# A graph network on one core: half of a comparison matrix moved from VectorE to ScalarE in every fourth tick of the first convolution, and one index write moved with it

## The chip, the core and the metric

The kernel runs on one core of a Trainium2 chip. The metric is the device time in microseconds (us) of one execution; the kernel before was timed in 3 runs. A core has five engines with a queue each, and each works its queue strictly in the order in which the program issued it: TensorE (PE, with its weight loads shown as PEld), VectorE (DVE), ScalarE (ACT), GpSimd (POOL) and SyncE (SP), the last of which only issues DMAs here.

## The reference

There are 12500 nodes with 64 features and 200000 edges, sorted by destination. Two graph convolutions over the nodes come first (a mean over the incoming edges, two 64x64 products, a bias), then a message step over the edges, whose results are averaged by `src`.

```python
h = jnp.maximum(_layernorm(x), 0.0)
agg = jax.ops.segment_sum(h[src], dst, num_segments=N)       # first convolution
cnt = jax.ops.segment_sum(jnp.ones(E), dst, num_segments=N)
h = relu(agg / maximum(cnt, 1)[:, None] @ W1l.T + b1 + h @ W1r.T)
...                                                          # second convolution, the same without relu
x = x + out
h = jnp.maximum(_layernorm(x), 0.0)
m = relu(concat([h[src], h[dst], edge_attr]) @ W1 + b1) @ W2 + b2
return x + segment_mean(m, src)
```

## The kernel before, in words

**Blocks and cells.** The nodes are cut into 49 blocks of 256. An edge belongs to a cell (destination block B, source block k), so there are 49 x 49 = 2401 cells, each with 128 slots. A sort (`sort(B)`, inside `made_cells`) puts the edges of destination block B into their cells. It runs on DVE and PE beside the first convolution, one block ahead, in 13 steps a block, which `sort_to` deals out by the number of cells done (about one step in a tick).

**Ticks of a convolution.** `some_cells` handles G = 4 cells, which this text calls a tick; a convolution has 601 ticks, the last with a single cell. A tick gathers source rows by multiplying a 0/1 matrix `turned` (made by DVE, L735) with the node table on PE (L890, tile `got`, four PSUM banks, two for a tick); ACT casts the result into `rows` (L894, two casts a tick). Then `hot` (L744, DVE) builds a second 0/1 matrix: for each of the four cells 256 columns, 1 where the slot's local destination number (`dcol`) equals the column. Three ticks later (`yield` three times) `Sums.add` multiplies `hot` by `rows` on PE (L769) into the block's sums `acc`.

**The end of a block.** When the 49 cells of a block are summed, `conv` goes on in the following ticks: ACT copies the sums (L810), DVE adds and scales them (L814 to L822), PE transposes them (L828), ACT copies the transposed block (L830, `both_t`), PE multiplies it by the weights in the next tick (L833), DVE adds the bias in the same tick (L835, `conv`), and ACT and DVE make the next table from that (L841 and L346 to L352).

**The order inside a tick.** For every engine the order of issue is: first the new tick's gather, casts and `hot`; then one step of each older tick and block in `line` (sums, `conv`); then the sort's steps (`sort_to`); then zeroing DMAs; then one step of `turned` for the next 16 cells; last a step of `edge_terms` (`beside`), which from cell 150 on computes the edge features' share of the messages: PE transposes (L402), an ACT copy (L408), PE products (L417), an ACT copy (L425, `terms_o`, three buffers), an ACT copy of positions (L379), and eight indirect DMAs on POOL (L385) that scatter the results to memory.

**The sort's positions.** In the sort's step with the first half of the products L639, DVE computes `pos_f` from the ranks (L644) and then writes it, scaled and as int32, to `pos` or `pos_late` (L645). Those positions are read by L379 only, many ticks later. In the next sort step ACT copies the products (L650, L651 to `scol`, L653 to `dcol`).

**The second convolution and the message stage** follow. The message stage already makes half of its own such matrices on ACT (`hot_a`): one `Abs` for each cell with the slot's number as bias (L1091), and one `Relu` over four cells (L1093), so that 1 - 2|column - number|, cut at zero, is 1 on equality and 0 elsewhere.

Of the kernel before, what the change touches and what calls it, by code (L numbers as in the profile page):

```python
# [12 lines left out]
AF = mybir.ActivationFunctionType  # L13
OP = mybir.AluOpType
# [100 lines left out]
def fast_path(  # L115
# [19 lines left out]
    nc = tc.nc  # L135
# [5 lines left out]
    NB = -(-N // BLK)  # L141
# [39 lines left out]
    G = 4  # L181
# [19 lines left out]
    for s, xs in enumerate(xs_all):  # L201
        full = min((s + 1) * CH, FULL) - s * CH
# [24 lines left out]
    every = consts.tile([P, 2 * P], BF, name="every")  # L227
# [18 lines left out]
    bias = []  # L246
# [50 lines left out]
    dcol = consts.tile([P, CELLS + 1], BF, name="dcol")  # L297
# [206 lines left out]
    def pos_of(B):  # L504
        return pos[:, B] if B < EARLY else pos_late[:, B - EARLY]
# [3 lines left out]
    def made_cells(work, psum):  # L509
# [60 lines left out]
        def pairs(a):  # L570
            return a.rearrange("p (g c) -> p g c", c=2)

        def mid(a, n):

            return a.unsqueeze(2).to_broadcast([a.shape[0], a.shape[1], n, 2])

        def lead_(a, n):

            return a.unsqueeze(1).to_broadcast([a.shape[0], n, a.shape[1], 2])

        def earlier(a, n):

            (row, _), (step, _) = a.ap
            return bass.AP(a.tensor, a.offset, [[row, P], [2 * step, TG], [2 * step, n], [step, 2]])

        def sort(B):

            keyed, shifted, slo, dlo = batch[B]
            kv = keyed[:, T:]
            odd = T // 2  # L590
            KE = NB + T - 1

            v = work.tile([P, TG, 3, NB, 2], BF, name="hot3", bufs=1)
            nc.vector.tensor_tensor(v[:, :, 0], mid(pairs(kv), NB), lead_(kexp, TG), op=OP.is_equal)  # L594
            yield
            p = psum.tile([P, 512], FT, name="pX")
            q = p[:, :2 * NB].rearrange("p (k c) -> p k c", c=2)
            for g in range(TG):
                nc.tensor.matmul(q, lead, v[:, g, 0], start=g == 0, stop=g == TG - 1)
            r = work.tile([P, TG, KE, 2], BF, name="ranks", bufs=1)  # L600
            nc.vector.tensor_tensor(r[:, :, NB:NB + odd], mid(pairs(kv), odd), earlier(shifted, odd), op=OP.is_equal)
            nc.vector.tensor_tensor(r[:, :, NB + odd:], mid(pairs(kv), T - 1 - odd),
                                    earlier(keyed[:, 2:], T - 1 - odd), op=OP.is_equal)
            yield
            nc.vector.tensor_mul(v[:, :, 1], v[:, :, 0], mid(pairs(slo), NB))
            yield
            ahead_p = work.tile([P, NB, 2], BF, name="ahead_p", bufs=1)
            with nc.allow_low_precision(reason="integers up to 256 are exact"):
                nc.vector.tensor_reduce(ahead_p, q.unsqueeze(2).to_broadcast([P, NB, 2, 2]), AX.X, OP.add)
            nc.vector.tensor_mul(r[:, :, 0:NB], v[:, :, 0], lead_(ahead_p, TG))  # L610
            yield
            nc.vector.tensor_mul(v[:, :, 2], v[:, :, 0], mid(pairs(dlo), NB))
            yield
            k = KE
            for n in range(3):
                h = k - k // 2
                nc.vector.tensor_tensor(r[:, :, 0:k - h], r[:, :, 0:k - h], r[:, :, h:k], op=OP.add)  # L617
                k = h
                if n == 1:
                    yield  # L620
            rb = work.tile([P, T], BF, name="rank_b", bufs=1)
            with nc.allow_low_precision(reason="integers up to 256 are exact"):
                nc.vector.tensor_reduce(pairs(rb), r[:, :, 0:k].rearrange("p g k c -> p g c k"), AX.X, OP.add)
            nc.vector.tensor_max(most, most, rb)
            halves = []
            for g0, g1 in ((0, (TG + 1) // 2), ((TG + 1) // 2, TG)):
                yield
                hot = work.tile([P, (TG + 1) // 2, S, 2], BF, name="hot_r")
                nc.vector.tensor_tensor(hot[:, :g1 - g0], mid(pairs(rb)[:, g0:g1], S), lead_(rexp, g1 - g0),  # L629
                                        op=OP.is_equal)  # L630
                halves.append((g0, g1, hot))
            yield
            p = psum.tile([P, 512], FT, name="pX")
            for g0, g1, hot in halves:
                yield

                for g in range(g0, g1):
                    for c in range(2):
                        nc.tensor.matmul(p[:, :2 * NB].rearrange("p (v k) -> p v k", v=2), hot[:, g - g0, :, c],  # L639
                                         v[:, g, 1:3, :, c], start=g + c == 0, stop=g + c == TG)  # L640
                if g0 == 0:
                    j, n, f = table_of(B)
                    q = work.tile([P, T], FT, name="pos_f", bufs=1)
                    nc.vector.scalar_tensor_tensor(q, rb, float(NB), kv, op0=OP.mult, op1=OP.add)  # L644
                    nc.vector.tensor_scalar(pos_of(B), q, float(n), float(n * NB + f),  # L645
                                            op0=OP.mult, op1=OP.add)
            n, f = place[B]
            F = len(order[n])
            cols = work.tile([P, 2 * NB], BF, name="cols_o")
            nc.scalar.copy(cols, p[:, :2 * NB])  # L650
            nc.scalar.copy(scol[:, scol_at[n]:scol_at[n] + NB * F].rearrange("p (k f) -> p k f", f=F)[:, :, f],  # L651
                           p[:, 0:NB])
            nc.scalar.copy(dcol[:, B * NB:(B + 1) * NB], p[:, NB:2 * NB])  # L653
            yield
            p = psum.tile([P, 512], FT, name="pX")
            pt = p.bitcast(BF)[:2 * NB, 0:S]
            nc.tensor.transpose(pt, cols, ident_b)
            o = work.tile([2 * NB, S], BF, name="rows_o", bufs=1)
            nc.scalar.copy(o, pt)
            nc.sync.dma_start(srow_b[B].rearrange("(k s) -> k s", s=S), o[0:NB])  # L660
            nc.sync.dma_start(srow_k[n][:, f * S:(f + 1) * S], o[0:NB])
            nc.sync.dma_start(drow_k[n][:, f * S:(f + 1) * S], o[NB:2 * NB])
            yield
# [19 lines left out]
        p = psum.tile([P, 512], FT, name="pX")  # L683
# [19 lines left out]
    with tc.tile_pool(name="raw_ps", bufs=1, space=bass.MemoryType.PSUM) as raw_ps:  # L703
        for n, raw in enumerate(raws):
            p = raw_ps.tile([P, D], FT, name="pW", bufs=2)
# [34 lines left out]
    def hot(work, cols, bufs, g=G):  # L740

        o = work.tile([P, g // 2, 2 * P, 2], BF, name="hot", bufs=bufs)
        n = cols.shape[1] // 2
        nc.vector.tensor_tensor(  # L744
            o[:, :n],
            cols.rearrange("p (g c) -> p g c", c=2).unsqueeze(2).to_broadcast([P, n, 2 * P, 2]),
            local.rearrange("p h q c -> p (h q) c").unsqueeze(1).to_broadcast([P, n, 2 * P, 2]),
            op=OP.is_equal)
        return o
# [44 lines left out]
    def even(a, z):  # L794
        return slice(a, z + (z - a) % 2)

    psum = ctx.enter_context(tc.tile_pool(name="sums_ps", bufs=2, space=bass.MemoryType.PSUM))
    sums = Sums(psum)
    layers = ExitStack()
    gather = layers.enter_context(tc.tile_pool(name="gather_ps", bufs=4, space=bass.MemoryType.PSUM))  # L800
    work = layers.enter_context(tc.tile_pool(name="layers", bufs=2))
# [79 lines left out]
    def some_cells(layer, t, c0, a, z):  # L881
        n = z - a
        table = (ta, tb)[layer]
        g = next_rows()
        for c in range(0, n, 2):
            m = min(2, n - c)
            p = gather.tile([P, 512], FT, name="got")
            for i in range(c, c + m):
                for h in range(2):
                    nc.tensor.matmul(p[:, (i - c) * D3:(i - c + 1) * D3],  # L890
                                     t[:, h, (a - c0 + i) * S:(a - c0 + i + 1) * S],
                                     table[:, (a + i) % NB, h], start=h == 0, stop=h == 1,
                                     skip_group_check=True)
            nc.scalar.copy(g[:, c:c + m, :D3], p[:, :m * D3].rearrange("p (c d) -> p c d", c=m))  # L894
        o = hot(work, dcol[:, even(a, z)], 5)
        yield
        yield
        yield
        full = []
        sums.add(o, g, a, z, lambda *a: full.append(a))  # L900
        for B, acc in full:
            yield from conv(layer, table, wcat[layer], bias[layer],
                            (after_conv1, after_conv2)[layer], B, acc)
# [67 lines left out]
    work = ctx.enter_context(tc.tile_pool(name="last", bufs=2))  # L971
# [186 lines left out]
    while summed:  # L1158
        f, args = summed.pop(0)
# [262 lines left out]
```

## Time and profile before

| what | value |
|---|---|
| median of 3 runs | 3682.99 us (3680.9 to 3687.05) |
| profiled execution | 3679.43 us, span of its instructions 3677.6 us |
| mean granted TensorE clock | 0.988 |
| first convolution, from its first gather to its last tick | 90.6 to 1306 us of the span |
| second convolution | to about 2275 us, message stage to the end |
| busy in the span | PE 93%, weight loads 92%, DVE 89%, ACT 68%, POOL 73% |

A busy share is a mean over stages. The lines by window, by waits and in order of time, which the prediction shows, say what holds each stage.

### The profile page before, as it was taken

How to read it: one execution, taken by the hardware profiler on the slowest of the kernel's cores; microseconds unless marked ns; L12 is line 12 of the kernel's file. 1: busy time of each engine (PE TensorE's matmuls, PEld its weight loads, DVE VectorE, ACT ScalarE, POOL GpSimd, SP SyncE). 2: the span in 40 equal slices, each digit the busy share in tenths (PEclk: the TensorE clock that was granted, in tenths of full speed). 3: DMA queues.
4: the chain of work that ended last, by engine and by line, in shares of the span. 5: the costliest groups of instructions: out<-in, count | busy, mean ns of one | idle time of the engine just before them, and what ended most of it. 6: DMA issues, size and time to landing. Idle time of an engine off the chain costs nothing.

```text
span 3677.6 us, 126942 instructions
## 1 busy us (share of the span) xinstructions
PE 3425.8 (93%) x50925; PEld 3367.7 (92%) x50925; DVE 3269.0 (89%) x5738; ACT 2506.9 (68%) x5949; POOL 2698.3 (73%) x2305
## 2 busy tenths in 40 slices
PE   1799999999899999999999998999999999999987
PEld 0788989898889999999999997999999999999887
DVE  7999999999999978788788787899889998998998
ACT  3455656565556667777777775788888888887665
POOL 4067787777777877777777773788888888887444
PEclk9999999999999999999999999999999999999999
DMA  6754545554454434444444444666766666666664
GB/s 211 268 164 150 169 152 163 155 161 151 147 168 145 128 125 142 132 137 147 136 131 137 140 134 144 224 214 200 218 212 211 204 214 214 207 207 206 194 211 140
DMA packets 413671, 635.66 MB, mean 173 GB/s; under 512 B 94131, under 2 KB 296247, under 8 KB 413070
## 3 DMA queue, kind: packets, MB, share of 16 engines
q1 hardware_dynamic: 353106, 572.87, 49.4%
q0 software_dynamic: 53312, 51.36, 4.1%
q8 instruction: 399, 6.54, 0.7%
q10 hardware_dynamic: 6652, 3.24, 0.4%
q14 instruction: 202, 1.65, 0.1%
HBM read 474.72 MB, written 155.83 MB: 171 GB/s over the span
## 4 chain that ended last, share of the span: by engine, by line
PE 64%; DVE 25%; DMA 5%; issue 3%; POOL 2%; SPq 1%; ACT 1%; DVEq 0%; ACTq 0%; POOLq 0%
PE acc L769 23%; PE got L890 13%; PE got L1071 12%; PE got L1072 6%; DVE hot L744 6%; DVE turned L735 4%; PE pE L417 3%; DVE hot_r L629 3%; PE pE L402 2%; DVE ranks L617 1%; DVE turned_d L735 1%; POOL terms L385 1%; DMA terms<-tb 1%; DMA terms_in<-terms 1%; DVE hot L594 1%
## 5 line engine op out<-in xcount | busy, mean ns | idle before, releaser
L385 POOL DMA_INDIRECT terms<-terms_o,turn_i x1666 | 1904.0, 1143 | 649.9 <-issue 427.8
L894 ACT CAST rows<-got 128x384 bf16<-128x384 f32 x2402 | 1038.4, 485 | 657.2 <-PE got L890 642.6
L769 PEld LDWEIGHTS <-hot 128*128 128x128 bf16 x12006 | 1032.5, 99 | 13.5 <-issue 4.0
L769 PE MATMUL acc<-rows,hot 128*128 128x193 bf16 x9604 | 1010.8, 248 | 0.0
L1083 POOL TENSOR_TENSOR hidden<-hidden 128x512 f32<-128x512 f32 (+1 forms) x602 | 756.4, 1256 | 265.1 <-ACT hidden L1080 179.5
L890 PEld LDWEIGHTS <-turned 128*128 128x128 bf16 x9604 | 814.6, 98 | 88.1 <-DVE turned L735 58.9
L744 DVE TENSOR_TENSOR hot<-dcol,local 128x1024 bf16<-128x1024 bf16 x1202 | 807.5, 682 | 9.0 <-PE acc L769 8.1
L735 DVE TENSOR_SCALAR turned<-srow,nid 128x2048 bf16<-128x2048 bf16 (+1 forms) x906 | 777.6, 872 | 20.7 <-issue 10.6
L1071 PE MATMUL got<-ta,turned 128*128 128x128 bf16 x3920 | 600.1, 221 | 7.3 <-DVE turned L735 7.3
L1071 PE MATMUL got<-tb,turned_d 128*128 128x128 bf16 x3920 | 600.6, 221 | 1.1 <-DVE turned_d L735 0.8
L890 PE MATMUL got<-ta,turned 128*128 128x192 bf16 x4802 | 510.5, 249 | 71.5 <-DVE turned L735 47.9
L1072 PE MATMUL got<-tb,turned_d 128*128 128x64 bf16 x3920 | 546.3, 193 | 0.0
L1072 PE MATMUL got<-ta,turned 128*128 128x64 bf16 x3920 | 546.1, 193 | 0.0
L1091 ACT ACTIVATE hot_a<-every,scol 128x256 bf16<-128x256 bf16 x1200 | 507.0, 493 | 0.0
L890 PE MATMUL got<-tb,turned 128*128 128x192 bf16 x4802 | 494.4, 246 | 0.9 <-DVE turned L735 0.5
L1080 ACT ACTIVATE hidden<-y 128x512 f32<-128x512 f32 (+1 forms) x301 | 190.4, 633 | 272.5 <-DVE y L1077 156.2
L1071 PEld LDWEIGHTS <-turned 128*128 128x128 bf16 x3920 | 362.1, 98 | 8.2 <-issue 7.8
L1071 PEld LDWEIGHTS <-turned_d 128*128 128x128 bf16 x3920 | 359.5, 98 | 1.7 <-DVE turned_d L735 1.7
L1072 PEld LDWEIGHTS <-turned 128*128 128x128 bf16 x3920 | 359.4, 98 | 1.2
L1072 PEld LDWEIGHTS <-turned_d 128*128 128x128 bf16 x3920 | 359.9, 98 | 0.0
L1093 ACT ACTIVATE hot_a<-hot_a 128x1024 bf16<-128x1024 bf16 x300 | 317.2, 1057 | 9.5
L735 DVE TENSOR_SCALAR turned_d<-drow,nid 128x2048 bf16<-128x2048 bf16 (+2 forms) x302 | 320.2, 1101 | 0.0
(217 smaller groups left out, 4898.1 us busy)
## 6 DMA issues: line engine op xcount, KB each, us to landing
srow<-srow_b SPq DMA_DIRECT2D x300, 512.0 KB
srow<-srow_k SPq DMA_DIRECT2D x149, 512.0 KB
drow<-drow_k SPq DMA_DIRECT2D x149, 512.0 KB
terms_in<-terms SPq DMA_DIRECT2D x294, 160.0 KB
edges<-in_edge_attr_dram SPq DMA_DIRECT2D x200, 192.0 KB
terms<-tb SPq DMA_DIRECT2D x200, 160.0 KB
terms<-tb SPq DMA_DIRECT2D x48, 640.0 KB
terms<-terms_o,turn_i POOLq DMA_INDIRECT x1666
```

The lines of the kernel that those rows point to most:

```text
L385: nc.gpsimd.indirect_dma_start(out=terms[j][:], out_offset=bass.IndirectOffsetOnAxis(ap=at[:, c, h:h + 1], axis=0), in_=o[:, c, h], in_off ...
L735: nc.vector.tensor_scalar(o[:, h, :n * S], r[:, :n * S], nid[:, h:h + 1], None, op0=OP.is_equal)
L744: nc.vector.tensor_tensor(o[:, :n], cols.rearrange("p (g c) -> p g c", c=2).unsqueeze(2).to_broadcast([P, n, 2 * P, 2]), local.rearrange(" ...
L769: nc.tensor.matmul(self.acc[B][:, h, :W3], lt, r[:, c, 0:W3], start=k + h == 0, stop=k == row - 1 and h == 1, skip_group_check=True)
L890: nc.tensor.matmul(p[:, (i - c) * D3:(i - c + 1) * D3], t[:, h, (a - c0 + i) * S:(a - c0 + i + 1) * S], table[:, (a + i) % NB, h], start=h ...
L894: nc.scalar.copy(g[:, c:c + m, :D3], p[:, :m * D3].rearrange("p (c d) -> p c d", c=m))
L1071: nc.tensor.matmul(p[:, c], lt, rt[:, 0:2 * D], start=i == 0, stop=False, skip_group_check=True)
L1072: nc.tensor.matmul(p[:, c, 0:D], lt, rt[:, 2 * D:], start=False, stop=i == 3, skip_group_check=True)
L1080: nc.scalar.activation(w[:, :n, 0:D], y[:, :n], AF.Relu)
L1083: nc.gpsimd.tensor_sub(w[:, :n, (i + 1) * D:(i + 2) * D], w[:, :n, j], upper(w)[:, :n, j])
L1091: nc.scalar.activation(q[:, c - k], every, AF.Abs, scale=-1.0, bias=scol[:, scol_at[last] + a + c:scol_at[last] + a + c + 1])
L1093: nc.scalar.activation(q[:, :n - k], q[:, :n - k], AF.Relu, bias=1.0, scale=-2.0)
```

## The change

Two edits. In the first convolution (`layer == 0`), in every fourth tick (`a // G % 4 == 1`, 150 ticks), DVE compares two cells only, into the first half of the `hot` tile. The other two cells are made by ACT into the second half, each cell contiguous: two `Abs` of 256 columns and one `Relu` over both. `Sums.add`, which already had the argument `q` for such a half, takes its last two cells from there. And the write of the sort's positions (L645), once for each of the 49 blocks, goes from DVE to ACT as one `Copy` activation with scale and bias. Nothing else is moved.

```diff
                     nc.vector.scalar_tensor_tensor(q, rb, float(NB), kv, op0=OP.mult, op1=OP.add)
-                    nc.vector.tensor_scalar(pos_of(B), q, float(n), float(n * NB + f),
-                                            op0=OP.mult, op1=OP.add)
+                    nc.scalar.activation(pos_of(B), q, AF.Copy, scale=float(n), bias=float(n * NB + f))
...
-        o = hot(work, dcol[:, even(a, z)], 5)
+        q = None
+        if layer == 0 and n == G and a // G % 4 == 1:
+            whole = hot(work, dcol[:, a:a + 2], 5)
+            o, q = whole[:, :1], whole[:, 1].rearrange("p q c -> p (q c)").rearrange("p (c q) -> p c q", c=2)
+            for c in range(2):
+                nc.scalar.activation(q[:, c], every, AF.Abs, scale=-1.0, bias=dcol[:, a + 2 + c:a + 3 + c])
+            nc.scalar.activation(q, q, AF.Relu, bias=1.0, scale=-2.0)
+        else:
+            o = hot(work, dcol[:, even(a, z)], 5)
         yield
         yield
         yield
         full = []
-        sums.add(o, g, a, z, lambda *a: full.append(a))
+        sums.add(o, g, a, z, lambda *a: full.append(a), q=q)
```

## The prediction

> **What bounds the kernel now.** I read the page first. PE is the busiest engine over the span, but DVE, from which work is taken, is close behind, so the question is what holds the first convolution alone.
>
> ```profile
> PE 3425.8 (93%) x50925; PEld 3367.7 (92%) x50925; DVE 3269.0 (89%) x5738; ACT 2506.9 (68%) x5949; POOL 2698.3 (73%) x2305
> ...
> L1091 ACT ACTIVATE hot_a<-every,scol 128x256 bf16<-128x256 bf16 x1200 | 507.0, 493 | 0.0
> L1093 ACT ACTIVATE hot_a<-hot_a 128x1024 bf16<-128x1024 bf16 x300 | 317.2, 1057 | 9.5
> ```
>
> Second, the busy time by stretches of 100 us: one of the first convolution and one of the second.
>
> ```profile
> core 0: us, PE busy (x) PEld busy (x) DVE busy (x) ACT busy (x) POOL busy (x), PEclk, DMA share, GB/s
> 400.00:500.00 100.00, 94.49 (x1164) 91.89 (x1163) 98.55 (x185) 62.09 (x169) 82.02 (x60) 1.00 0.53 161
> 1500.00:1600.00 100.00, 100.00 (x1135) 98.67 (x1134) 79.01 (x177) 73.14 (x203) 78.06 (x72) 1.00 0.41 134
> ```
>
> The two convolutions have different limits. The second is PE's, with DVE at 79%. In the first DVE is at 98.55% and PE has some 8% to spare (weight loads 91.89 against 98.67). So DVE time saved there counts, and at most those 8% can be won before PE is the bound. ACT is at 62%.
>
> Third, the waits between 200 and 1250 us (total us, times, longest).
>
> ```profile
> ACT rows L894 <- PE got L890: 320.2, 343, 6.0
> POOL terms L385 <- issue: 185.8, 606, 1.0
> ...
> PEld L890 <- DVE turned L735: 50.0, 42, 3.9
> ...
> ACT terms_o L425 <- DMA terms<-terms_o,turn_i: 30.0, 16, 4.3
> ...
> DVE conv L835 <- PE acc L833: 16.2, 14, 3.3
> ```
>
> PE waits for DVE (50 us), ACT waits for PE (320 us), and DVE waits for almost nothing. So PE and ACT run ahead of DVE in the order of issue and DVE sets the pace. POOL is near a limit too: after each of its DMAs it spends 0.30 us in issue (185.8 / 606), and 60 DMAs in 100 us make 18 us, which with the 82.02 busy fills the stretch. ACT's 30 us for a `terms_o` buffer are POOL's backlog showing.
>
> Fourth, the order of time around one block's end of sort (start, us, what), because the change puts a wait on ACT there.
>
> ```profile
> 905.98 0.86 ACT L894 CAST rows<-got 128x384 bf16<-128x384 f32 x2 [0.81 <-PE got L890]
> ...
> 906.73 0.61 ACT L408 COPY edges_t<-pE 128x512 f32<-128x512 f32 x1
> ...
> 908.15 0.86 ACT L894 CAST rows<-got 128x384 bf16<-128x384 f32 x2 [0.82 <-PE got L890]
> ...
> 908.89 0.39 ACT L830 COPY both_t<-acc 128x256 f32<-128x256 f32 x1
> ...
> 911.65 0.19 DVE L644 SCALAR_TENSOR_TENSOR pos_f<-rank_b,keys 128x34 f32<-128x34 bf16 x1
> 911.69 0.53 PEld L833 LDWEIGHTS acc<-wcat,both_t 128*128 128x128 f32 x4
> ...
> 911.87 0.18 DVE L645 TENSOR_SCALAR pos<-pos_f 128x34 int32<-128x34 f32 x1
> ...
> 913.17 0.28 DVE L835 TENSOR_TENSOR conv<-acc,bias 128x128 f32<-128x128 f32 x1
> ```
>
> By the order of issue the new ACT write of `pos` stands between the casts of 905.98 and the copy L408 of 906.73. Its input `pos_f` comes from DVE's L644, which ends at 911.84. ACT is there 5.0 us before DVE.
>
> **The change part by part.** Sums are against the profiled execution, 3679.4 us (span 3677.6); the median of the runs is 3.6 us higher.
>
> *Half of hot leaves DVE.* A full `hot` of 128x1024 takes 0.683 us, and the one tick with a single cell pair (128x512) took 0.420 in the groups by form. Half saves 0.263, in 150 ticks 39.5 us, all of it on an engine that sets the pace: **-39.5 us**.
>
> *L645 leaves DVE.* 49 x 0.182 us: **-8.9 us**.
>
> *Half of hot arrives on ACT.* Two `Abs` of 128x256 at 0.493 (L1091), and a `Relu` of 128x512; the only row of that size, L1080 with f32, has 0.634, and between L1091 and L1093 the bounds are 0.493 and 1.057. I take 0.634, the nearest shape. That makes 1.62 us a tick, 243 us in all, and ACT goes from 62% to about 82% of the stage. Where it only delays casts it costs nothing: the sums use `rows` three ticks (about 6 us) after the casts began, and PE may gather two ticks ahead with its four `got` banks. If that cover were gone, PE would wait up to 1.6 us in each of 150 ticks.
>
> The skill's page "ScalarE: Activation LUTs", section "Rules for kernel authors", advises against this edit: relu and its like belong on VectorE, which is up to about 3 times faster in bf16. The rows say worse, 1.62 against 0.263 us, or 6 times; at 3 times the ACT part would be 0.79 us and the total below 15 us lower (18 paths x 0.83). The rows decide.
>
> *The write of `pos` on ACT.* The operation itself is bounded by L379 (128x8, 0.218) and L653 (128x49, 0.335); I take 0.22, which leaves at most 0.12 x 46 = 5 us above. What counts is its wait. Taking for each of blocks 3 to 48, as in the lines above, the time from the end of the casts before the slot to the end of L644, ACT would stand 0.7 to 10.0 us, 4.4 us in the mean, 201 us in all. Behind it stand `edges_t` or `terms_o`, the next casts, and L830. PE's L833 waits for L830, and DVE's L835 for L833. So a chain is closed that was open: DVE L644 to ACT to PE to DVE L835. It can't be hidden by a lead of ACT or PE, since it starts at DVE's own instruction.
>
> I add it up for each block: 0.22, ACT's busy time from the slot to the end of L830, 1.62 where a tick with the new half lies between, and 0.68 for L833 with the hand-over. Against it stands the present time from the end of L644 to the start of L835, less what DVE saves in between (L645, a shorter `hot`). Four patterns occur, by the ticks of casts in between:
>
> - one tick, no new half: 16 blocks, chain 2.50 us against 1.99;
> - one tick with one: 6 blocks, 4.28 against 2.22;
> - two ticks, none: 12 blocks, 4.68 against 3.15;
> - two ticks with one: 12 blocks, 6.41 against 3.34.
>
> In block 34, above: 0.22 + 1.96 + 0.69 = 2.87 after 911.84, so DVE could start L835 1.7 us later than its 913.17 less 0.18. The positive differences sum to 12.5 + 12.4 + 19.7 + 36.8: **+81.5 us** of new DVE waiting. The trace has such a stall already: near 822, 851 and 651 us ACT stood 2.9, 4.3 and 4.2 us for a `terms_o` buffer, and the next L835 waited 3.3, 2.6 and 2.5 us for L833. Over the stage 30.0 us of such ACT waits stand beside 16.2 us of L835 waits. By that ratio 201 us of waiting would cost 109 us, which I keep as the upper end. The lower end is zero, or a gain, if DVE finds other work in its queue ready; it doesn't reorder, so I don't take that.
>
> *The weight loads* of the contiguous half: L769 loads from `hot_a` take 96 ns, from `hot` 98. 600 of them are 1 us on PE, which isn't the bound.
>
> *POOL.* From its first DMA at 200 us on POOL never waits for ACT by more than 1.2 us. A faster stage would only fill its backlog sooner, so it caps gains (see the rivals); a slower one costs it nothing. SP issues nothing new; the sort's row writes (L660) go out a few us later, but stand 8 to 12 us before the loads that read them.
>
> Sum: -39.5 - 8.9 + 81.5 = **+33 us**, 3712 on the profiled execution, 3716 beside the median. With the chain's ends, L835 waits between 60 and 109 us, it is 3695 to 3745.
>
> The page "SBUF — State Buffer", section on the "DVE blocks DMA" trap, says that POOL can't write descriptors while VectorE holds a port pair they share. POOL's mean is 1.19 us in 800 to 1000 (157.84 / 133) and 1.09 in 1800 to 2000 (145.54 / 133), where DVE is less busy. By the rule a lighter DVE quickens POOL, which changes nothing here unless POOL is the bound.
>
> **The rivals.** *Faster, held by POOL* (0.20). The chain hides, because L835 has slack in DVE's queue that I don't see, and the 48 us come through until POOL stops them. The point from which it decides is a chain no longer than DVE's own 2 to 3.5 us after L644. POOL's string of DMAs runs from 200 to beyond 1310 us with 0.3 us gaps; with three buffers the copy that ends at 1314 can't come more than about 3.5 us earlier, about 3 more from ticks before POOL starts, and up to 22 us if POOL quickens (4/17 of the 0.13 us between its stage means 1.23 and 1.10, on some 720 DMAs). So 6 to 28 us: 3655 to 3677. For it: DVE is at 98% and loses real work. Against it: the queue order. The full 48 us need POOL out of the way as well.
>
> *No difference* (0.07). The stall eats just the saving: chain costs of 41 to 56 us. For it: most blocks' single-tick pattern is short.
>
> *Much slower, ACT as the bound* (0.18). ACT's 82% and 4.4 us a block of waiting (18% of 24 us) fill it, casts fall behind by more than the two ticks of `got` banks, PE waits too: 109 - 48 = +60, 3743, and beyond. Against: ACT's wait shrinks as its other work grows.
>
> **How the numbers follow.** A measurement of this kernel can tell about 0.2%, 7 us. The likeliest case, slower by the chain (0.55), gives 3716; its own range is 3695 to 3745. Faster 0.20, same 0.07, slower 0.55 + 0.18 = 0.73. The range to hold 8 in 10 takes in most of the faster rival and most of the worst case: 3660 to 3765.
>
> **What would show it.** In the profile after, ACT's `pos` write should wait on DVE `pos_f` L644, 100 to 210 us in total; DVE's L835 should wait on PE L833 60 to 110 us instead of 16; DVE's busy share in the stage should fall from 98 to 92 or 93%; the ACT half should read 0.49, 0.49 and 0.63 us; the stage should end at about 1340 us; ACT's waits for `terms_o` should shrink. I am wrong if L835's waits stay under 40 us, or if the stage ends before 1300 us with POOL filled throughout.

## The result, and the profile after

The changed kernel takes 3716.5 us (median of 4 runs, 3710.98 to 3717.23) against 3681.94 us (4 runs) for the kernel before: a ratio of 1.0086, 95% interval 1.0074 to 1.0099. The forecast was 3716. The profiled execution is 3715.9 us long with a span of 3714.1, which is 36.5 us over the span before. The last tick of the first convolution starts at 1339.1 us instead of 1306.1, so 33.0 us of that have arisen by there, 1.7 of them before the stage's first gather (92.3 us instead of 90.6); under 1 us comes in the second convolution and the rest after it.

The busy time of that stage, by window, before and after (the same columns as in the prediction):

```profile
90.00:1306.00 1216.00, 1110.93 (x13468) 1080.36 (x13469) 1162.50 (x2224) 712.29 (x1908) 874.56 (x717) 0.98 0.52 162
```

```profile
92.00:1339.00 1247.00, 1123.86 (x13468) 1088.81 (x13469) 1118.28 (x2176) 901.11 (x2404) 884.33 (x719) 0.98 0.50 158
```

The third pair is DVE's. Its work falls by 44.2 us (1162.50 to 1118.28), but the stage grows by 31, so its idle time goes from 53.5 to 128.7 us. The edit did what it says, and 75 us of new idling are more than it saved. DVE's busy share of the stage goes from 95.6% to 89.7%. ACT's busy time, the fourth pair, grows by 189 us, from 59% to 72% of the stage.

Where DVE idles now, and what else changed, by the waits between 200 and 1290 us of the kernel after (L893, L829, L832, L834 are L894, L830, L833, L835 of before):

```profile
...
POOL terms L385 <- ACT turn_i L379: 133.1, 11, 116.0
ACT pos L645 <- DVE pos_f L644: 124.7, 34, 7.0
ACT rows L893 <- PE got L889: 121.5, 185, 3.1
DVE conv L834 <- PE acc L832: 53.4, 27, 3.2
PEld acc L832 <- ACT both_t L829: 33.4, 27, 4.5
...
ACT pos_late L645 <- DVE pos_f L644: 24.2, 8, 4.1
...
DVE conv L834 <- ACT rows L893: 18.1, 13, 3.8
```

ACT stands 149 us (124.7 + 24.2) at the write of the positions. PE's L832 now waits for ACT's `both_t`, which is nowhere among the longer waits of before, and DVE's bias addition L834 waits 53.4 us for PE and 18.1 us where the last semaphore is put down to ACT: 71.5 us instead of 16.5. The chain ACT, PE, DVE shows link by link. ACT's waits for a `terms_o` buffer, 30.0 us before, are gone from the list. Over the whole stage L834's waits come to 79.6 us where they were 23.0. So the chain is 57 of the new idling; DVE's waits for ACT at `three_r` and `tb` (L348, L352) add 15 (4.2 to 19.0) and those for the DMA of `srow` 8 (3.0 to 11.2), less a few us elsewhere.

Block 34 in order of time, to be laid beside the same block of before:

```profile
933.06 0.85 ACT L893 CAST rows<-got 128x384 bf16<-128x384 f32 x2
...
937.61 0.19 DVE L644 SCALAR_TENSOR_TENSOR pos_f<-rank_b,keys 128x34 f32<-128x34 bf16 x1
...
937.83 0.23 ACT L645 ACTIVATE pos<-pos_f 128x34 int32<-128x34 f32 x1 [3.92 <-DVE pos_f L644]
937.97 0.57 ACT L408 COPY edges_t<-pE 128x512 f32<-128x512 f32 x1
938.44 0.86 ACT L893 CAST rows<-got 128x384 bf16<-128x384 f32 x2
939.18 0.39 ACT L829 COPY both_t<-acc 128x256 f32<-128x256 f32 x1
...
939.62 0.66 PE L832 MATMUL acc<-wcat,both_t 128*128 128x64 f32 x4 [1.72 <-ACT both_t L829]
...
940.39 0.29 DVE L834 TENSOR_TENSOR conv<-acc,bias 128x128 f32<-128x128 f32 x1 [1.38 <-ACT rows L893]
```

ACT waits 3.92 us for `pos_f`; then its next three steps run back to back, PE had stood 1.72 us, and L834, whose wait the profile puts down to `rows` though L832 ended only 0.11 us before it (at 940.28), starts 2.59 us after L644's end (937.80) where it started after 1.33 us before. The sum in the prediction had 2.87 us for this block.

### The profile page after: what moved, and what is told of

Same layout as the page of the kernel before. It is cut to its first block, busy times and chain, and to the rows that moved or that the text cites. A ratio compares the mean times of both kernels' runs of the same rounds, so it can differ in the third digit from the quotient of the medians.

```text
span 3714.1 us, 126737 instructions
## 1 busy us (share of the span) xinstructions
PE 3437.3 (93%) x50925; PEld 3374.9 (91%) x50925; DVE 3237.8 (87%) x5689; ACT 2697.0 (73%) x6448; POOL 2718.2 (73%) x2305
## 4 chain that ended last, share of the span: by engine, by line
PE 62%; DVE 19%; DMA 6%; issue 5%; ACT 3%; POOL 3%; SPq 1%; ACTq 0%; POOLq 0%; DVEq 0%
PE acc L768 22%; PE got L889 13%; PE got L1078 12%; PE got L1079 6%; DVE hot L743 4%; PE pE L417 4%; DVE turned L734 3%; POOL terms L385 3%; DVE hot_r L629 2%; PE pE L402 2%; DMA terms<-terms_o,turn_i 1%; DVE ranks L617 1%; ACT rows L893 1%; DVE turned_d L734 1%; PE acc L832 1%
## 5 line engine op out<-in xcount | busy, mean ns | idle before, releaser
L385 POOL DMA_INDIRECT terms<-terms_o,turn_i x1666 | 1926.2, 1156 | 670.3 <-issue 426.1
L893 ACT CAST rows<-got 128x384 bf16<-128x384 f32 x2402 | 1038.5, 488 | 416.2 <-PE got L889 407.9
L734 DVE TENSOR_SCALAR turned<-srow,nid 128x2048 bf16<-128x2048 bf16 (+1 forms) x906 | 781.8, 877 | 27.4 <-DMA srow<-srow_b 11.2
L743 DVE TENSOR_TENSOR hot<-dcol,local 128x1024 bf16<-128x1024 bf16 (+1 forms) x1202 | 768.8, 650 | 8.1 <-PE acc L768 7.4
L734 DVE TENSOR_SCALAR turned_d<-drow,nid 128x2048 bf16<-128x2048 bf16 (+2 forms) x302 | 321.4, 1106 | 0.6 <-DMA drow<-drow_k 0.6
```

The source lines that it names most:

```text
L385: nc.gpsimd.indirect_dma_start(out=terms[j][:], out_offset=bass.IndirectOffsetOnAxis(ap=at[:, c, h:h + 1], axis=0), in_=o[:, c, h], in_off ...
L734: nc.vector.tensor_scalar(o[:, h, :n * S], r[:, :n * S], nid[:, h:h + 1], None, op0=OP.is_equal)
L743: nc.vector.tensor_tensor(o[:, :n], cols.rearrange("p (g c) -> p g c", c=2).unsqueeze(2).to_broadcast([P, n, 2 * P, 2]), local.rearrange(" ...
```

## The experiments

Theory A: the wait of the ACT write of `pos` closes a chain from DVE over ACT and PE back to DVE, and that is what costs. Rival B: the cost is ACT's load. Theory C, the cap that the prediction put on gains: POOL's string of scatters. Kernels that ran together share the runs of the kernel before: 3683.28 us beside the first four, 3683.0 beside the next four, 3690.59 beside the last two.

**Hot alone on ACT** (positions by `nc.vector.tensor_scalar` as before).

```diff
-                    nc.scalar.activation(pos_of(B), q, AF.Copy, scale=float(n), bias=float(n * NB + f))
+                    nc.vector.tensor_scalar(pos_of(B), q, float(n), float(n * NB + f),
+                                            op0=OP.mult, op1=OP.add)
```

> Half of hot on ScalarE as in the change, the positions written by VectorE as before. Theory A (the ACT write of pos closes a chain VectorE, ScalarE, TensorE, VectorE in each block): no chain is left, the 39.5 us of VectorE work come through until POOL's scatters stop them, so 3655 to 3680 us, L835's counterpart waits for TensorE stay at about 20 us. Rival B (the cost is ScalarE's load of 1.6 us in every fourth tick): about as slow as the changed kernel, 3700 to 3716 us.

Measured: 3689.44 us, ratio 1.0017 (1.0005 to 1.0029). Both expectations missed. The cost of the whole change is mostly gone without the positions' write, against B, but the 39.5 us don't come through either, against A as priced. The waits between 200 and 1290 us say where they went:

```profile
...
PEld pE L402 <- ACT terms_o L425: 52.1, 39, 4.5
ACT terms_o L425 <- DMA terms<-terms_o,turn_i: 46.3, 28, 5.1
PE pE L402 <- ACT terms_o L425: 43.6, 36, 4.3
DVE conv L835 <- PE acc L833: 37.9, 24, 4.2
```

ACT waits 46.3 us for a scatter to free a `terms_o` buffer (30.0 before), PE waits behind ACT for the bank `pE`, and DVE's L835 stands 37.9 us. It is the same path back to DVE, with another wait at its head. POOL's queue has no room meanwhile: between 202 and 1318 us its 717 DMAs take 881.5 us, the gaps after them 194.9 and its waits for its own earlier DMAs 22.2, together 1099 of 1116 us (before, between 200 and 1306 us: 875.2, 195.6 and 19.3, or 1090 of 1106). The stage's last tick starts 12 us later than before.

**The positions alone on ACT** (hot wholly on DVE).

> Only the positions' write on ScalarE, hot wholly on VectorE. Theory A: the chain without the new half between, 46 us by the sum over the blocks and about two thirds of that by what came in the changed kernel, less 8.9 us: 3702 to 3719 us, with 30 to 46 us of waiting at the bias addition (L834). Rival B: ScalarE has only 11 us more to do and VectorE 9 us less, so 3674 to 3684 us.

Measured: 3711.95 us, ratio 1.0081 (1.0058 to 1.0104), as A has it and not B. In its waits between 200 and 1290 us:

```profile
...
ACT pos L645 <- DVE pos_f L644: 165.2, 34, 8.3
...
ACT pos_late L645 <- DVE pos_f L644: 38.9, 9, 5.5
...
DVE conv L834 <- PE acc L832: 35.9, 25, 4.7
...
DVE conv L834 <- ACT rows L893: 10.9, 12, 1.9
```

Moving 49 instructions of 0.18 us, 8.9 us of work, costs 29 us with the saving taken off: L834 waits 46.8 us, just above the 30 to 46 expected, where it waited 16.5. ACT waits longer here (204 us) than with the whole change (149), which fits its having less else to do.

**The whole change, positions written late.** The instruction is unchanged, but issued in the next block's sort, six steps later by the order of the steps.

```diff
+        unwritten = []
+
+        def write_pos():
+            while unwritten:
+                o, i, scale, bias = unwritten.pop()
+                nc.scalar.activation(o, i, AF.Copy, scale=scale, bias=bias)
+
...
             nc.vector.tensor_mul(r[:, :, 0:NB], v[:, :, 0], lead_(ahead_p, TG))
+            write_pos()
             yield
...
-                    nc.scalar.activation(pos_of(B), q, AF.Copy, scale=float(n), bias=float(n * NB + f))
+                    unwritten.append((pos_of(B), q, float(n), float(n * NB + f)))
...
         assert sorted_to[0] == STEPS * NB
+        write_pos()
```

> The whole change, but ScalarE writes a block's positions about eight sort steps later, in the next block's sort, when pos_f has long been there. All instructions are the same in number and size. Theory A: ScalarE's waits for pos_f go from 149 us to nearly none, and the time to that of hot alone or a few us below, 3650 to 3678 us. Rival B: the load is unchanged, so 3705 to 3717 us.

Measured: 3703.02 us, ratio 1.0056 (1.0039 to 1.0072), between the two: 25 us above A's range and 2 below B's. The waits between 200 and 1290 us:

```profile
...
ACT terms_o L425 <- DMA terms<-terms_o,turn_i: 55.2, 30, 5.4
...
DVE conv L843 <- PE acc L841: 49.1, 28, 5.3
...
DVE conv L843 <- ACT rows L902: 7.1, 3, 3.3
```

ACT's waits for `pos_f` are gone, and 13 us with them; but ACT's waits for `terms_o` rise to 55.2 us and L843 (L835 of before) still waits 56 us. The stage is POOL's, as with hot alone: its DMAs, the gaps after them and its waits for its own DMAs fill 1106 of the 1127 us from 200 to 1327. That it is 14 us slower than hot alone, with 8.9 us less DVE work, neither theory foresaw. By itself this run doesn't decide between A and B.

**The late write with an even pace** of the edge features' steps, which gives POOL fewer scatters in a tick of the first convolution and more in the second.

```diff
-                beside.passed((z - a) * (1.1, 0.9)[layer])
+                beside.passed((z - a) * (1.0, 1.0)[layer])
```

> As the late write, and the edge features' steps dealt out evenly over both convolutions (1.0 and 1.0 a cell instead of 1.1 and 0.9). Theory C (POOL's string of scatters caps the first convolution): ScalarE's waits for terms_o buffers vanish and it is 10 to 25 us faster than the late write alone. If POOL is no cap: within 5 us of it.

Measured: 3677.76 us, ratio 0.9982 (0.997 to 0.9995): 25 us faster than the late write alone, as C has it, at the upper end of its 10 to 25. The waits between 200 and 1290 us:

```profile
...
PEld L898 <- DVE turned L743: 39.7, 34, 3.7
...
DVE conv L843 <- PE acc L841: 19.5, 23, 2.2
```

PE waits for DVE's `turned` again and L843 is down to 19.5 us; no wait for `terms_o` buffers is left in the list, and the last tick of the stage starts 31.8 us earlier than before (in a profiled execution of 3668.78 us, the second fastest of the ten).

**The kernel before with the even pace**, a control.

> The kernel before with the even pace of the edge features' steps (1.0 and 1.0). Control for the next two. If POOL is a cap only for a lighter VectorE, the first convolution gains 10 to 20 us here (16 us of VectorE's waits and the ScalarE waits for terms_o), and the second loses about as much as with the late write (18 us, PE being full there): 3675 to 3692 us.

Measured: 3700.04 us, ratio 1.0043 (1.0027 to 1.0059), beyond the expectation. In the profiled executions (3699.92 against 3679.43 us) the stage gains 8.5 us and what follows loses 29: PE is full in the second convolution (busy 100.00 of the 100 us from 1500), and ACT waits 27.5 us there for `terms_o` buffers (2.8 between 1300 and 2200 us before), so the cap had moved with the pace.

**The whole change with the even pace.**

> The whole change with the even pace: POOL is no cap, so against the late write at this pace (3678 us) only the place of the positions' write differs. Theory A (the chain): 40 to 60 us slower than that, 3715 to 3738 us, or somewhat less as far as PE work moved out of the stage relieves the chain (not below 3700). Rival: if the wait of ScalarE is harmless and POOL explained it all, 3675 to 3685 us.

Measured: 3726.46 us, ratio 1.0122 (1.0098 to 1.0145). The waits of this kernel between 200 and 1290 us:

```profile
...
ACT pos L645 <- DVE pos_f L644: 131.8, 34, 7.3
...
DVE conv L834 <- PE acc L832: 49.9, 33, 2.8
PEld acc L832 <- ACT both_t L829: 34.9, 31, 2.8
```

It differs from the late write at this pace in nothing but the place of 49 instructions in ACT's queue, neither has a wait for `terms_o` buffers among the longer waits of the first convolution, and it is 48.7 us slower (3726.46 - 3677.76). In the profiles all of that arises in the first convolution, as the gathers of the two kernels show (shortest, median and longest in ns, start of the first and of the last), here and with the late write:

```profile
L889 PE MATMUL got<-ta,turned x4802: 243/246/368, 92.1 to 1329.5; 128*128 128x192 bf16 x193
```

```profile
L898 PE MATMUL got<-ta,turned x4802: 243/246/368, 90.7 to 1274.4; 128*128 128x192 bf16 x193
```

That is the price of the chain where POOL has room, and A is shown. At the old pace, where POOL holds the stage, the same step was worth 13.5 us (3716.5 - 3703.02).

**Hot alone with the even pace.**

> Half of hot on ScalarE, positions on VectorE, even pace. If the 39.5 us come through once POOL has room: the first convolution 23 to 40 us shorter than in the kernel before, within 10 us of the late write at this pace (31.8 us shorter), the total 3676 to 3688 us. If ScalarE's load eats it: the total no better than the control.

Measured: 3671.48 us, ratio 0.997 (0.9958 to 0.9982), 28.6 us under the control and 4.5 below the expected range; its stage is 25.7 us shorter than in the kernel before, as expected. Less the control's 8.5, some 17 of DVE's 39.5 us come through in the stage itself (23 with the late write). That is nearly all of the 18.9 us between the profiled executions, of which this one (3681.04 us) was the slowest of its seven; where its faster executions gain the other 10 no profile shows. ACT's load doesn't eat the saving, and B falls here.

**The late write with 1.05 and 0.95.**

> The late write with a pace between (1.05 and 0.95). The first convolution keeps POOL just filled, the second loses half as much as at 1.0: 3665 to 3678 us. If POOL's cap bites at once below 1.1 to 1.05, 3685 us or more.

Measured: 3678.0 us, ratio 0.9979 (0.9969 to 0.999), at the expectation's upper edge. ACT still waits 22.8 us for `terms_o` in the first convolution: at 1.05 POOL is just overfilled.

**A trimmed pace**, 1.0 and 0.97, with hot alone and with the late write.

> Half of hot on ScalarE, positions on VectorE, the edge features' steps at 1.0 and 0.97 a cell. At 1.0 in the second convolution ScalarE waited 15 to 18 us there for terms_o buffers, so POOL caps that stage too. If that is what it lost: 5 to 12 us faster than with 1.0 (3671 us), 3658 to 3668 us. If the loss is only the PE work moved there: within 4 us of 3671.

> The same pace with the whole change and the late write of the positions. If the late write saves VectorE its 8.9 us: 3 to 9 us faster than hot alone at this pace. If it is worth nothing, or less, as at the old pace: 0 to 10 us slower.

Measured: 3666.16 us for hot alone, ratio 0.9929 (0.9915 to 0.9943), and 3662.58 us for the late write, ratio 0.9921 (0.9907 to 0.9935). Both beat the kernel before and the changed one; the first expectation is met, the second with 3.6 us at its lower end. The kernel before ran 7.6 us longer beside these two than beside the four above, so how much the trimming brought to hot alone lies between 5 us by the times and 15 by the ratios. In the late write's waits between 1320 and 2250 us there is none for `terms_o` buffers among the longer ones. The late write was 13.6 us worse than hot alone at the old pace, 6.3 worse at the even one and 3.6 better here. Against the spread of the runs (3664 to 3681 us for one kernel of these) only the first is clear, and why it was worse there stays open; POOL's string ended later in that trace, with a mean DMA about as long (1234 ns against 1229).

## Why the prediction was right

*Half of hot leaves DVE*: said 39.5 us, from 0.263 us a tick; the two-cell `hot` took 0.417 us, and with L645 DVE's work in the stage fell by 44.2 of the 48.4 us counted.

*The chain*: said 81.5 us of new waiting, with 60 to 109 as ends for L835's waits. DVE's idle time grew by 75 us; L834's waits between 200 and 1290 us grew by 55 us, to 71.5. Taking the chain from DVE's instruction on, and not from ACT's arrival, was what kept it near. But the term stood for L835 alone, and over the whole stage L834 took 57 of the 75 us. The rest it had priced at nothing: 15 us where DVE waits for ACT at `three_r` and `tb` (the sum has no term for a later ACT there), and 8 at the loads of `srow` (whose writes were to stand 8 to 12 us ahead of them). So the total of +33 us came out closer than its terms: the chain was some 25 us too dear, these two were missing, and DVE's work fell 4 us less than counted. That they cancel is luck; the path and its sign are not. The other price, in proportion to ACT's waiting (201 us by 16.2 / 30.0), was too high: from block 3 on ACT waited 169 us, and even for those the ratio gives 91 us of new waiting at L834.

*The stage's end*: said about 1340 us, measured 1339.1. *DVE's share* was to fall from 98 to 92 or 93% and fell from 95.6 to 89.7: the fall is as said, but 98 was that of a single stretch. *ACT's rows*: `Abs` 0.52 and `Relu` 0.63 us, said 0.49 and 0.63. *ACT's load* was mis-sized: 72% of the stage, where the sum had 82%. It had started from the 62% of one stretch, where the stage before has 58.6% (712.29 of 1216 us), and the stage grew. Two `Abs` in a row take 0.92 us and not 0.99, and ACT instructions that follow one another without a wait overlap a little (L893 starts 0.10 us before L408 ends in block 34), so that 244 us of added rows became 189 busy. The outcome didn't hang on it.

*The rule on ScalarE*: by the Trainium skill's page "ScalarE: Activation LUTs", section "Rules for kernel authors", relu and its like belong on VectorE, which per element is up to about 3 times faster in bf16. Here the same two cells cost 1.55 us on ACT, in three instructions (0.92 + 0.63), and 0.27 on DVE (0.684 - 0.417), nearly 6 times. It didn't decide, though: with the wait gone and POOL given room, the edit that breaks the rule is worth 28.6 us, because ACT had idle time and DVE had next to none.

*The faster rival, held by POOL*, was half right. The cap is real: hot alone gained nothing. Of its price, 6 to 28 us of gain, up to 22 counted on POOL growing quicker with a lighter DVE, and that step fell; the other 6 did not come either. POOL's busy time in the stage, by the groups of lines, before and with hot alone:

```profile
L385 POOL DMA_INDIRECT terms<-terms_o,turn_i x717 | 875.2, 1221 | 345.4 <-issue 195.6 <-ACT turn_i L379 115.9 <-DMA terms<-terms_o,turn_i 19.3
```

```profile
L385 POOL DMA_INDIRECT terms<-terms_o,turn_i x717 | 881.5, 1229 | 350.4 <-issue 194.9 <-ACT turn_i L379 116.8 <-DMA terms<-terms_o,turn_i 22.2
```

The same 717 DMAs take 1221 and 1229 ns in the mean, with 38 us less DVE work beside them. The Trainium skill's page "SBUF — State Buffer" (the "DVE blocks DMA" trap) names DVE instructions that use two ports; whether `hot` is one that holds POOL back no run here shows, and taking some of it away didn't help POOL. Why POOL's DMAs are shorter in the second convolution (1.09 us against 1.19) stays open: not only DVE is less busy there, the mean DMA share is lower too (0.43 against 0.49).

*Much slower, ACT as the bound*, did not come: ACT has 28% of the stage left.

## What to carry to other kernels

Before an instruction moves to another engine, look at how far that engine runs ahead of the producer of its input: a 0.2 us write that stood 4 us ahead of its data cost 29 to 49 us over 49 blocks where nothing else held the stage (13.5 where POOL did), and nothing clear of the spread of the runs once it was issued six steps later and POOL had room. Price such a wait by the path that leads back to the bounding engine, from the producer's end through what is queued behind the waiting instruction, and not by the length of the wait. When work leaves the bounding engine, ask which queue fills next even if it looks 80% busy; here a string of short DMAs with 0.3 us between them was full at that share.

## What the runs showed that was not expected

POOL's issue gap of 0.3 us makes 60 to 69 indirect DMAs in 100 us a full queue, though its busy share in such stretches reads 77 to 82%. And the wait of ACT for a buffer of POOL's takes the same road to DVE as the wait for `pos_f`: 30.0 us of it stood beside 16.2 us at L835, 46.3 us beside 37.9.
